# Two graph layers on one core: weight sums moved, background work spread differently, a bias added by DMA, and the layer boundary reordered

## The chip, the cores and the metric

The kernel runs on one core of a Trainium2 chip. Its time is what the device takes for one execution, in microseconds. A measurement is the median of a few executions. The profile and the trace come from one further execution, taken by the hardware profiler, whose own time stands beside its span in the table below.

A core has a matrix engine (TensorE, "PE" in the profile, its weight loads "PEld"), three engines for elementwise work (VectorE "DVE", ScalarE "ACT", GpSimd "POOL") and SyncE ("SP"), which here only issues DMAs. Each engine takes its own instructions in order. The engines meet through semaphores.

## The reference

There are N = 2708 rows of D = 1024 floats and an integer matrix adj of N x N. Both layers normalize first and add their result to x.

```python
# layer 0
h = jnp.maximum(_layernorm(x, axis=-1), 0.0)
f = h @ Wf + bf
g = h @ Wg + bg
e = jax.nn.relu(f @ g.T)
attention = jax.nn.softmax(jnp.where(adj > 0, e, NEG), axis=1)
x = x + attention @ (h @ W + bW)
# layer 1
h = jnp.maximum(_layernorm(x, axis=-1), 0.0)
k = h @ W1
f1 = k @ a1
f2 = k @ a2
e = leaky_relu(f1 + f2.T, 0.2)
attention = jax.nn.softmax(jnp.where(adj > 0, e, NEG), axis=1)
x = x + relu(attention @ k)
```

## The kernel before, in words

**Products.** All matrix products are float32. Each is computed with the Strassen-Winograd scheme: the operands are cut into 2 x 2 blocks, and seven products of half size (M1 to M7) of sums of blocks take the place of eight. The sums are made by DVE or POOL. The results are put together where PSUM is emptied, which is called an eviction. [...]

**Tiles.** The rows are 22 tiles, 20 of 128 rows and two of 74. They go in eleven pairs. The N rows of the output of a layer are also cut into five panels of 586, 586, 512, 512 and 512. Matrices are kept transposed, so a panel is a range of columns of a transposed score matrix, and every product has a half panel (293 or 256) or 512 as its free size.

**Stages of layer 0.** f and g are not computed. Wf times the transpose of Wg is folded into one matrix, and `project_q(p)` multiplies it with panel p of h. For each panel p, `scores(p)` then multiplies every pair of row tiles with that result. It writes seven products for a pair, adds the mask and keeps the running maximum. Then come `project_q(p+1)` and `aggregate(0, p)`, which multiplies the softmax weights with h, and `project(0, p)`, which multiplies by W and adds the residual. The order is broken at the end: `project(0, 3)` stands after `scores(4)`, and `project(0, 4)` comes last of layer 0, working on one pair after the other (`by_pair`).

**Stages of layer 1.** The scores need no matrix product. f1 and f2 are two dot products per row (`dots(0)`, `dots(1)`), made when a row of layer 0 is done. `mx[p]` collects the column maximum for panel p (`raise_max`, one DVE instruction for each row tile and panel). `shifts1(p)` makes of it the shift of the softmax: `column_max` turns `mx[p]` on TensorE, reduces it on DVE, and a chain of nine operations of 128 x 5 follows. `weights1(p)` spreads two results over the partitions (`spread`: transpositions on TensorE into PSUM and a copy out). For each row tile it then makes the weights P by an Identity on ACT (L1144), two operations on DVE and an Exp on ACT (L1147). Then `aggregate(1, p)` and `project(1, p)` follow for each panel.

**Masks.** While layer 0 computes its scores, adj is loaded as integers, converted by DVE (`convert`, tile nm), turned by TensorE (`turn`, mk_ps, L615), copied by ACT (L616) and stored to mk_d. Layer 1 loads masks from there.

**Order of the work.** A list named `later` holds background work with a nominal duration each: the layernorms, the sums of W, dots, maxima, softmax steps. `behind(rate)` stands in the products and lets as much of the list go as its credit pays for. `flush()` empties the list. In `scores` `behind` is called with seven rates for each pair, and the rate was 0.6 for panel 0 and 1.0 for the rest (L901). A scheduler then orders the instructions of each engine. It is bound to program order for SP's loads (`load`, L120), and for DVE inside `scores` alone (`nc.hold`). Nearly all DVE instructions show as L44, where a helper records them.

**Queues.** All loads are issued by SP in program order. All stores are issued by POOL. Buffers that loads share come from a ring of twelve (`stream`), others from a pool of 54 (`slot`). A load waits for what last used its buffer, and so do all loads behind it on SP.

**What the change touches.**
- `prepare_W` (called at L1110) puts eight pieces of work in the list. Each loads two rows of blocks of W (w_rows), makes four sums on DVE and stores them to wt_d (L775), and for layer 1 also makes four dot products.
- `finish0(p)`: `start` loads the residual x_res and adds the bias row bwb on POOL (L1078). `go` adds an evicted result (L1082) and stores the row to x1_d (L1083, "x_d" in the profile).
- `project`: M1 is copied out of PSUM by ACT (L827), M5 and M6 are added to it, and M3, M7 and M4 each take two DVE additions, one to the stored sum and one to the residual.
- `rows_done` for the last panel: it normalizes the row in place (ACT, L251), which must wait for the store of that row. It then makes both dots and the maximum.

Of the kernel before, what the change touches and what calls it, by code (L numbers as in the profile page):

```python
# [56 lines left out]
def kernel(  # L57
# [141 lines left out]
    def halves(t):  # L199
        return [t[:, e * W:(e + 1) * W] for e in range(2)]  # L200
# [38 lines left out]
        nc.scalar.activation(rs[:n, :1], mv[:n, 1:2], AF.Sqrt, bias=eps[:n])  # L239
        of_rows[id(t)] = mv, rs  # L240

    def normalize(t):

        n = t[0].shape[0]
        if id(t) not in of_rows:
            moments(t)
        mv, rs = of_rows.pop(id(t))
        nc.vector.reciprocal(rs[:n, :1], rs[:n, :1])
        nc.vector.tensor_scalar(rs[:n, 1:], mv[:n, :1], rs[:n, :1], -1.0, op0=OP.mult, op1=OP.mult)
        for e in range(2):  # L250
            nc.scalar.activation(t[e], t[e], AF.Relu, bias=rs[:n, 1:], scale=rs[:n, :1])  # L251

    def pair_h(l, q, ha, hb):

# [532 lines left out]
    def project(l, p, G, finish, then={}, by_pair=False, rate=2.0):  # L787

        full = width[p] // P
        col = lambda i, n: [t[:, :, i * P:i * P + n] for t in G]  # L790
        todo = [(first[p] + i, first[p] + i + 1, P, col(i, P), col(i + 1, P)) for i in range(0, full, 2)]
        if p == panel_of[short[0]]:
            n = tiles[short[0]][1]
            for e in range(2):
                nc.scalar.copy(carry[:, e, :, :n], G[e][:, :, full * P:full * P + n])
        if p == panel_of[short[1]]:
            n = tiles[short[1]][1]
            todo.append((*short, n, [carry[:, e, :, :n] for e in range(2)], col(full, n)))
        start_of, finish = finish
        ws = {m: load_W(l, m) for m in (M1, M2)}  # L800
        start_of([t for g in todo for t in g[:2]])
        lefts = []
        for ta, tb, n, (a11, a12), (a21, a22) in todo:
            s = [slot(f"ps{i}", (P, NH, P))[:, :, :n] for i in range(4)]
            add(s[0], a21, a22)
            sub(s[1], s[0], a11)
            sub(s[2], a11, a21)
            sub(s[3], a12, s[1])
            lefts.append({M1: a11, M2: a12, M5: s[0], M6: s[1], M7: s[2], M3: s[3], M4: a22})
        for group, left in (zip([[t] for t in todo], [[t] for t in lefts]) if by_pair else [(todo, lefts)]):  # L810
            acc, tmp = {}, {}
            for m in (M1, M2, M5, M6, M3, M7, M4):
                start = m in (M1, M5, M6)
                w_ = ws.pop(m) if m in ws else load_W(l, m)
                which = "x" if m in (M1, M2) else "y" if m in (M5, M3) else "z"
                for i, (ta, tb, n, _, _) in enumerate(group):
                    if start:
                        acc[which, i] = bank(f"p{which}")
                    ps = acc[which, i][:n]
                    for k in range(NH):  # L820
                        nc.tensor.matmul(ps, left[i][m][:, k, :], w_[k], start=(start and k == 0), stop=(k == NH - 1),  # L821
                                         skip_group_check=True)
                    if start:
                        tmp[m, i] = slot(f"pt{m}")
                    t = lambda m: tmp[m, i][:n, :W]
                    if m == M1:
                        nc.scalar.copy(t(M1), ps)  # L827
                    elif m == M2:
                        finish(ta, 0, ps)
                    elif m in (M5, M6):  # L830
                        add(t(m), ps, t(M1))
                    else:
                        o = {M3: M6, M7: M5, M4: M1}[m]
                        add(t(o), ps, t(o))
                        finish(tb if m != M3 else ta, 0 if m == M4 else 1, t(o))
                    behind(rate)
                if m in then:
                    then.pop(m)()
# [52 lines left out]
    def scores(p, B):  # L891
# [6 lines left out]
        spread(rb, [r_[:n, first[p] + i:first[p] + i + 1] for i, (_, n) in enumerate(panels[p])])  # L898
        acc = slot("acc")
        S = [None] * NT  # L900
        rate = 0.6 if p == 0 else 1.0  # L901
        lefts = {}

        def product(q, m, ps, start):
# [100 lines left out]
    def shifts1(p, between=None):  # L1005

        k, t0 = len(panels[p]), first[p]
        top = column_max(p, mx[p], between)[:, :k]
        f1 = f[0][:, t0:t0 + k]
        z, m, c = (stats.tile([P, 5], FP, name=nm)[:, :k] for nm in ("z", "m1", "none"))  # L1010
        nc.vector.tensor_add(z, f1, top)
        nc.vector.scalar_tensor_tensor(m, z, ALPHA, z, op0=OP.mult, op1=OP.max)
        nc.vector.tensor_scalar(c, top, -BIG / 2, None, op0=OP.is_ge)
        nc.vector.tensor_mul(m, m, c)
        nc.vector.tensor_scalar(c, top, -BIG / 2, -BIG, op0=OP.is_lt, op1=OP.mult)
        nc.vector.tensor_add(m, m, c)
        sub(z, f1, m)
        nc.vector.scalar_tensor_tensor(m, f1, ALPHA, m, op0=OP.mult, op1=OP.subtract)
        return z, m

    done_rows, first_mask = {}, {}

    def rows_done(t, xt):

        n = tiles[t][1]
        done_rows[t] = xt

        def dots(k):
            dot(f[k][:n, t:t + 1], xt, [b[:n] for b in halves(wab[k])])
            if k == 1:  # L1030
                nc.vector.tensor_scalar(f2s[:n, t:t + 1], f[1][:n, t:t + 1], ALPHA, None, op0=OP.mult)

        q, k = pair_of[t]
        whole = all(s in done_rows for s in pairs[q])
        if panel_of[t] == NP - 1:
            normalize(xt)
            dots(0)
            dots(1)
            raise_max(0, q, k, first_mask[t][:n, :width[0]])
            if whole and q == NQ - 1:  # L1040
                nc.scalar.activation(stats.tile([P, 1], FP, name="warm"), eps, AF.Exp)
            if whole:
                if q == NQ - 1:
                    got["zm"] = shifts1(0, lambda: pair_h(1, q, *(done_rows[s] for s in pairs[q])))
                else:
                    pair_h(1, q, *(done_rows[s] for s in pairs[q]))
                for p in range(1, NP):
                    put_max(p, q)
            return

        def met():
            known.add(q)
            for p in range(NP):
                if generated[p] > q:
                    put_max(p, q)
        put(1.5, lambda: moments(xt))
        put(0.5, lambda: normalize(xt))
        put(1.6, lambda: dots(0))
        put(1.6, lambda: dots(1))
        if whole:  # L1060
            put(2.7, lambda: pair_h(1, q, *(done_rows[s] for s in pairs[q])))
            put(0.0, met)

    def finish0(p):
        bwb = [slot(f"bwb{e}") for e in range(2)]
        for e in range(2):
            load(bwb[e][:, :W], bass.AP(tensor=bw.tensor, offset=bw.offset + e * W, ap=[[0, P], [1, W]]))
        xs, seen = {}, {}

        def start(ts):  # L1070
            for t in ts:
# [3 lines left out]
                xs[t] = row_halves("x_res", n, t in short)  # L1075
                for e in range(2):
                    load(xs[t][e], x[r0:r0 + n, e * W:(e + 1) * W])
                    nc.gpsimd.tensor_add(xs[t][e], xs[t][e], bwb[e][:n, :W])  # L1078

        def go(t, e, c):  # L1080
            n = tiles[t][1]
# [2 lines left out]
            seen[t] = seen.get(t, 0) + 1  # L1084
            if seen[t] == 2:
                rows_done(t, xs[t])
        return start, go

    got = {}
    generated = [0] * NP  # L1090

    def take_max(p):
        got["m"] = column_max(p, got["acc"])
# [6 lines left out]
    for p in range(NP):  # L1100
# [24 lines left out]
    project(0, NP - 1, G.pop(NP - 1), finish0(NP - 1), by_pair=True, rate=0.0)  # L1125


    def weights1(p, z, m):

        w = width[p]  # L1130
        ub, vb1, sm = slot("ub"), slot("vb1"), slot("sm")
        spread(ub, columns_of(p, z))
        spread(vb1, columns_of(p, m))
        S = [None] * NT
        order = [(q, k) for k in range(2) for q in range(NQ)]
        exps[0] = 0
# [1 line left out]
        def go(i, mk):  # L1138
            if i < len(order):
                q, k = order[i]  # L1140
                n, t = rows_of[q], pairs[q][k]
                S[t] = slot("P")
                s = S[t][:n, :w]
                nc.scalar.activation(s, vb1[:n, :w], AF.Identity, bias=f2s[:n, t:t + 1])  # L1144
                nc.vector.scalar_tensor_tensor(s, ub[:n, :w], f[1][:n, t:t + 1], s, op0=OP.add, op1=OP.max)
                add(s, s, mk[0][:n, :w])
                nc.scalar.activation(s, s, AF.Exp)  # L1147
            if i >= LAG:
                q, k = order[i - LAG]
# [3 lines left out]
        front = []  # L1153
        for i in range(len(order) + LAG):
            mk = []
            front.append([2.1, (lambda i=i, mk=mk: mk.append(load_mask(p, *order[i]))) if i < len(order) else None,
                          (lambda i=i, mk=mk: go(i, mk)), False, None])
        later[:0] = front
        return S, sm
# [1 line left out]
    def finish1(p):  # L1161
# [9 lines left out]
        def go(t, e, c):  # L1171
# [5 lines left out]
        return start, go  # L1177

    def take_shifts(p):
        flush()  # L1180
# [42 lines left out]
```

## Time and the profile before

| | |
|---|---|
| median of 3 executions | 3235.16 us (3231.14 to 3235.99) |
| profiled execution | 3237.23 us |
| its span | 3235.3 us |
| mean granted TensorE clock | 0.987 |
| PE busy | 3137.1 us (97%) |
| DVE busy | 1756.3 us (54%) |
| ACT busy | 507.7 us (16%) |
| POOL busy | 395.0 us (12%) |
| moved by DMA | 641.43 MB, mean 198 GB/s |

The busy shares are of the span. A group line of the profile gives the source line, the engine, the operation, output and input tiles, and shapes. A timeline line begins with the start and the duration in microseconds, and the bracket at its end gives the idle time of the engine just before it, and what ended that. A waits line gives the waiting instruction and what it waited for, the total in us, how often, and the longest. Where several matmuls follow one another, one timeline line holds them all.

### The profile page before, as it was taken

How to read it: one execution, taken by the hardware profiler on the slowest of the kernel's cores; microseconds unless marked ns; L12 is line 12 of the kernel's file. 1: busy time of each engine (PE TensorE's matmuls, PEld its weight loads, DVE VectorE, ACT ScalarE, POOL GpSimd, SP SyncE). 2: the span in 40 equal slices, each digit the busy share in tenths (PEclk: the TensorE clock that was granted, in tenths of full speed). 3: DMA queues.
4: the chain of work that ended last, by engine and by line, in shares of the span. 5: the costliest groups of instructions: out<-in, count | busy, mean ns of one | idle time of the engine just before them, and what ended most of it. 6: DMA issues, size and time to landing. Idle time of an engine off the chain costs nothing. (4 is left out here: it accounts for less than half of the span.)

```text
span 3235.3 us, 35363 instructions
## 1 busy us (share of the span) xinstructions
PE 3137.1 (97%) x12924; PEld 2333.4 (72%) x12924; DVE 1756.3 (54%) x3594; ACT 507.7 (16%) x853; POOL 395.0 (12%) x476
## 2 busy tenths in 40 slices
PE   8999999999999999999999998997999999999998
PEld 5577767667876578876888885864767748778585
DVE  7857594275812766327581358537574272553712
ACT  4412120010200102001020002003131030211200
POOL 3723110210002100021000101020010000000001
PEclk9999999999999999999999999998999999999999
DMA  6958866576445575457745565665555445555546
GB/s 262 332 174 297 276 229 227 171 243 215 141 130 163 173 247 190 151 191 242 228 156 156 165 209 185 225 237 200 198 161 175 148 159 171 186 189 175 194 150 212
DMA packets 279628, 641.43 MB, mean 198 GB/s; under 512 B 50686, under 2 KB 116178, under 8 KB 279456
## 3 DMA queue, kind: packets, MB, share of 16 engines
q1 hardware_dynamic: 245184, 525.56, 50.5%
q0 software_dynamic: 34272, 113.62, 9.4%
q8 instruction: 102, 1.67, 0.2%
q14 instruction: 70, 0.57, 0.1%
HBM read 525.49 MB, written 113.58 MB: 198 GB/s over the span
## 5 line engine op out<-in xcount | busy, mean ns | idle before, releaser
L917 PE MATMUL sz<-B,As 128*128 128x256 f32 (+3 forms) x1320 | 328.9, 399 | 5.3 <-DVE st L44 5.3
L917 PEld LDWEIGHTS sz<-B,As 128*128 128x128 f32 (+1 forms) x1320 | 248.7, 189 | 64.5 <-DVE st L44 6.4
L917 PE MATMUL sx<-B,As 128*128 128x256 f32 (+3 forms) x880 | 227.0, 401 | 14.2 <-DMA As<-hs_d 12.0
L756 POOL TENSOR_TENSOR gT<-gT,rr 128x2048 f32<-128x2048 f32 (+3 forms) x20 | 68.3, 3433 | 1320.5 <-DVE rr L44 700.2
L917 PE MATMUL sy<-B,As 128*128 128x256 f32 (+3 forms) x880 | 219.5, 392 | 0.0
L478 PE MATMUL gy<-T,hc 128*128 128x256 f32 (+3 forms) x880 | 205.7, 395 | 6.6 <-DMA hc<-hg_d 6.6
L478 PE MATMUL gx<-P,hc 128*128 128x256 f32 (+3 forms) x880 | 204.5, 394 | 4.7 <-ACT P L1147 4.7
L478 PE MATMUL gz<-Sa,hc 128*128 128x256 f32 (+3 forms) x880 | 206.6, 394 | 0.0
L478 PE MATMUL gz<-P,hc 128*128 128x256 f32 (+3 forms) x880 | 206.3, 393 | 0.0
L917 PEld LDWEIGHTS sx<-B,As 128*128 128x128 f32 (+1 forms) x880 | 162.3, 189 | 51.4 <-issue 11.2
L478 PEld LDWEIGHTS gy<-T,hc 128*128 128x128 f32 (+1 forms) x880 | 168.5, 192 | 42.3 <-DVE junk L44 4.4
L478 PEld LDWEIGHTS gx<-P,hc 128*128 128x128 f32 (+1 forms) x880 | 168.4, 192 | 40.9 <-ACT P L1147 5.0
L917 PEld LDWEIGHTS sy<-B,As 128*128 128x128 f32 (+1 forms) x880 | 163.9, 186 | 38.2 <-issue 0.9
L478 PEld LDWEIGHTS gz<-Sa,hc 128*128 128x128 f32 (+1 forms) x880 | 165.6, 190 | 31.8
L478 PEld LDWEIGHTS gz<-P,hc 128*128 128x128 f32 (+1 forms) x880 | 165.6, 190 | 31.8
L821 PE MATMUL px<-w,gT 128*128 128x512 f32 x320 | 147.3, 613 | 11.5 <-issue 10.0
L821 PE MATMUL py<-w,ps 128*128 128x512 f32 (+1 forms) x352 | 155.6, 593 | 0.3 <-DVE mcol L44 0.3
L821 PE MATMUL pz<-w,ps 128*128 128x512 f32 (+1 forms) x352 | 155.0, 592 | 0.0
L616 ACT COPY mask<-mk_ps 128x1024 bf16<-128x1024 bf16 (+1 forms) x55 | 55.6, 1011 | 575.8 <-PE mk_ps L615 254.6
L821 PEld LDWEIGHTS pz<-w,ps 128*128 128x128 f32 (+1 forms) x352 | 65.5, 186 | 85.6 <-issue 81.7
L821 PEld LDWEIGHTS py<-w,ps 128*128 128x128 f32 (+1 forms) x352 | 65.4, 186 | 85.6 <-issue 82.7
L821 PEld LDWEIGHTS px<-w,gT 128*128 128x128 f32 x320 | 62.5, 197 | 89.2 <-issue 85.3
(240 smaller groups left out, 4797.9 us busy)
## 6 DMA issues: line engine op xcount, KB each, us to landing
hc<-hg_d SPq DMA_DIRECT2D x350, 512.0 KB
As<-hs_d SPq DMA_DIRECT2D x150, 512.0 KB
w<-wt_d SPq DMA_DIRECT2D x96, 512.0 KB
w<-in_L_gnn_W_dram SPq DMA_DIRECT2D x72, 512.0 KB
md<-md_d SPq DMA_DIRECT2D x56, 512.0 KB
adj_i<-in_adj_dram SPq DMA_DIRECT2D x50, 512.0 KB
hg_d<-g POOLq DMA_DIRECT2D x40, 512.0 KB, 5.0
hs_d<-hsT POOLq DMA_DIRECT2D x40, 512.0 KB, 5.6
```

The source lines that it names most:

```text
L478: nc.tensor.matmul(ps[d], left(m, k, d), right(m, k), start=(start and k == 0), stop=(k == K - 1), skip_group_check=True)
L616: nc.scalar.copy(mk[:n, :, :k4 * P], ps[:n, :, :k4 * P])
L756: nc.gpsimd.tensor_tensor(of(e, s), of(e, s), by(s, k), OP.mult)
L821: nc.tensor.matmul(ps, left[i][m][:, k, :], w_[k], start=(start and k == 0), stop=(k == NH - 1), skip_group_check=True)
L917: nc.tensor.matmul(ps[:n, :h], lefts[q][:, i % 2, c, :n], B[m][c // 2][:, c % 2, :h], start=(start and c == 0), stop=(c == NH - 1), skip_g ...
```

## The change

1. `prepare_W` is called after M5 of `aggregate(0, 0)` instead of before that stage.
2. The rate in `scores` is 0.6, 1.0, 0.65, 0.65, 0.65 for the five panels instead of 0.6 and four times 1.0.
3. The bias row bW is not loaded to SBUF and added by POOL. Each x_res tile gets it by a DMA from POOL's queue that reads the row from DRAM for all partitions and adds it to what the tile holds.
4. In `project` of layer 0, as soon as M6 is there, `join` adds the three sums of M5, M6 and M1 to the residual tiles. M3, M7 and M4 are then added to the residual straight from PSUM. In the last panel M1 is copied by DVE instead of ACT.
5. In the last panel `normalize` writes into fresh tiles (h_last) instead of in place. `raise_max` stands between `dots(1)` and `dots(0)`. The small Exp that loads ACT's table is kept in program order ahead of them.
6. `scores_before` spreads f1 of panel 0 and makes, as background work behind `project(0, 3)`, the unshifted masked scores of panel 0 for the first tile of those nine pairs whose rows are both done by then. `weights1(0)` then subtracts the shift from these and applies Exp; the rest is made as before. `shifts1` returns this shift m as well.

```diff
-    def normalize(t):
+    def normalize(t, into=None):
...
-            nc.scalar.activation(t[e], t[e], AF.Relu, bias=rs[:n, 1:], scale=rs[:n, :1])
+            nc.scalar.activation((into or t)[e], t[e], AF.Relu, bias=rs[:n, 1:], scale=rs[:n, :1])
...
-        start_of, finish = finish
+        start_of, join, finish = finish
...
+        copy1 = nc.vector.tensor_copy if by_pair and l == 0 else nc.scalar.copy
...
+                    o = {M3: M6, M7: M5, M4: M1}.get(m)
                     if m == M1:
-                        nc.scalar.copy(t(M1), ps)
+                        copy1(t(M1), ps)
                     elif m == M2:
                         finish(ta, 0, ps)
-                    elif m in (M5, M6):
+                    elif o is None:
                         add(t(m), ps, t(M1))
-                    else:
-                        o = {M3: M6, M7: M5, M4: M1}[m]
+                    elif join is None:
                         add(t(o), ps, t(o))
                         finish(tb if m != M3 else ta, 0 if m == M4 else 1, t(o))
+                    else:
+                        finish(tb if m != M3 else ta, 0 if m == M4 else 1, ps)
+                    if join and m == M6:
+                        join(tb, 1, t(M5))
+                        join(ta, 1, t(M6))
+                        join(tb, 0, t(M1))
                     behind(rate)
...
-        rate = 0.6 if p == 0 else 1.0
+        rate = (0.6, 1.0, 0.65, 0.65, 0.65)[p]
...
         if panel_of[t] == NP - 1:
-            normalize(xt)
-            dots(0)
+            done_rows[t] = row_halves("h_last", n)
+            normalize(xt, done_rows[t])
+            if whole and q == NQ - 1:
+                tc.keep_in_program_order(nc.scalar.activation(stats.tile([P, 1], FP, name="warm"), eps, AF.Exp))
             dots(1)
             raise_max(0, q, k, first_mask[t][:n, :width[0]])
-            if whole and q == NQ - 1:
-                nc.scalar.activation(stats.tile([P, 1], FP, name="warm"), eps, AF.Exp)
+            dots(0)
...
-                    nc.gpsimd.tensor_add(xs[t][e], xs[t][e], bwb[e][:n, :W])
+                    nc.gpsimd.dma_start(xs[t][e], bass.AP(tensor=bw.tensor, offset=bw.offset + e * W, ap=[[0, n], [1, W]]),
+                                        accum_op=OP.add)
...
+        def join(t, e, c):
+            add(xs[t][e], xs[t][e], c)
+        return start, join, go
...
+    def scores_before():
+
+        w = width[0]
+        f1b = slot("f1b")
+
+        def go(q, mk):
+            n, t = rows_of[q], pairs[q][0]
+            before[t] = slot("P")
+            s = before[t][:n, :w]
+            nc.scalar.activation(s, f1b[:n, :w], AF.Identity, bias=f2s[:n, t:t + 1], scale=ALPHA)
+            nc.vector.scalar_tensor_tensor(s, f1b[:n, :w], f[1][:n, t:t + 1], s, op0=OP.add, op1=OP.max)
+            add(s, s, mk[0][:n, :w])
+        spread(f1b, columns_of(0, f[0]))
+        for q in range(NQ):
+            if panel_of[pairs[q][0]] < NP - 1 and panel_of[pairs[q][1]] < NP - 1:
+                mk = []
+                put(1.8, lambda q=q, mk=mk: go(q, mk), lambda q=q, mk=mk: mk.append(load_mask(0, q, 0)))
...
             project(0, p - 1, G.pop(p - 1), finish0(p - 1), hooks)
-        if p == 0:
-            prepare_W()
-        then = {}
+            scores_before()
+        then = {M5: prepare_W} if p == 0 else {}
...
+        if p == 0:
+            mb = slot("mb")
+            spread(mb, columns_of(p, shift))
+        else:
+            spreads()
...
-                S[t] = slot("P")
-                s = S[t][:n, :w]
-                nc.scalar.activation(s, vb1[:n, :w], AF.Identity, bias=f2s[:n, t:t + 1])
-                nc.vector.scalar_tensor_tensor(s, ub[:n, :w], f[1][:n, t:t + 1], s, op0=OP.add, op1=OP.max)
-                add(s, s, mk[0][:n, :w])
+                if p == 0 and t in before:
+                    S[t] = before.pop(t)
+                    s = S[t][:n, :w]
+                    sub(s, s, mb[:n, :w])
+                else:
+                    if p == 0 and not spreaded:
+                        spreads()
+                        spreaded.append(True)
...
                 nc.scalar.activation(s, s, AF.Exp)
```

More of the change, by code (lines that the diff above doesn't have):

```diff
@@ L1009, in shifts1 @@
         f1 = f[0][:, t0:t0 + k]
-        z, m, c = (stats.tile([P, 5], FP, name=nm)[:, :k] for nm in ("z", "m1", "none"))
+        z, m, c, d = (stats.tile([P, 5], FP, name=nm)[:, :k] for nm in ("z", "m1", "none", "m2"))
         nc.vector.tensor_add(z, f1, top)
+        nc.vector.tensor_scalar(c, top, -BIG / 2, None, op0=OP.is_ge)
+        nc.vector.tensor_scalar(d, top, -BIG / 2, -BIG, op0=OP.is_lt, op1=OP.mult)
         nc.vector.scalar_tensor_tensor(m, z, ALPHA, z, op0=OP.mult, op1=OP.max)
-        nc.vector.tensor_scalar(c, top, -BIG / 2, None, op0=OP.is_ge)
         nc.vector.tensor_mul(m, m, c)
-        nc.vector.tensor_scalar(c, top, -BIG / 2, -BIG, op0=OP.is_lt, op1=OP.mult)
-        nc.vector.tensor_add(m, m, c)
+        nc.vector.tensor_add(m, m, d)
         sub(z, f1, m)
-        nc.vector.scalar_tensor_tensor(m, f1, ALPHA, m, op0=OP.mult, op1=OP.subtract)
-        return z, m
+        nc.vector.scalar_tensor_tensor(c, f1, ALPHA, m, op0=OP.mult, op1=OP.subtract)
+        return z, c, m
     done_rows, first_mask = {}, {}
@@ L1028, in dots @@
         def dots(k):
-            dot(f[k][:n, t:t + 1], xt, [b[:n] for b in halves(wab[k])])
+            dot(f[k][:n, t:t + 1], done_rows[t], [b[:n] for b in halves(wab[k])])
             if k == 1:
@@ L1064, in finish0 @@
     def finish0(p):
-        bwb = [slot(f"bwb{e}") for e in range(2)]
-        for e in range(2):
-            load(bwb[e][:, :W], bass.AP(tensor=bw.tensor, offset=bw.offset + e * W, ap=[[0, P], [1, W]]))
         xs, seen = {}, {}
@@ L1086, in go @@
                 rows_done(t, xs[t])
-        return start, go
+        def join(t, e, c):
+            add(xs[t][e], xs[t][e], c)
+        return start, join, go
     got = {}
     generated = [0] * NP
+    before, spreaded = {}, []
+    def scores_before():
[13 more added lines that the diff above has]
+                put(1.8, lambda q=q, mk=mk: go(q, mk), lambda q=q, mk=mk: mk.append(load_mask(0, q, 0)))
     def take_max(p):
@@ L1125, with weights1, spreads @@
     project(0, NP - 1, G.pop(NP - 1), finish0(NP - 1), by_pair=True, rate=0.0)
-    def weights1(p, z, m):
+    def weights1(p, z, m, shift):
         w = width[p]
         ub, vb1, sm = slot("ub"), slot("vb1"), slot("sm")
-        spread(ub, columns_of(p, z))
-        spread(vb1, columns_of(p, m))
+        def spreads():
+            spread(ub, columns_of(p, z))
+            spread(vb1, columns_of(p, m))
+        if p == 0:
[3 more added lines that the diff above has]
+            spreads()
         S = [None] * NT
@@ L1141, in go @@
                 n, t = rows_of[q], pairs[q][k]
-                S[t] = slot("P")
-                s = S[t][:n, :w]
-                nc.scalar.activation(s, vb1[:n, :w], AF.Identity, bias=f2s[:n, t:t + 1])
-                nc.vector.scalar_tensor_tensor(s, ub[:n, :w], f[1][:n, t:t + 1], s, op0=OP.add, op1=OP.max)
-                add(s, s, mk[0][:n, :w])
+                if p == 0 and t in before:
[6 more added lines that the diff above has]
+                        spreaded.append(True)
+                    S[t] = slot("P")
+                    s = S[t][:n, :w]
+                    nc.scalar.activation(s, vb1[:n, :w], AF.Identity, bias=f2s[:n, t:t + 1])
+                    nc.vector.scalar_tensor_tensor(s, ub[:n, :w], f[1][:n, t:t + 1], s, op0=OP.add, op1=OP.max)
+                    add(s, s, mk[0][:n, :w])
                 nc.scalar.activation(s, s, AF.Exp)
@@ L1155, in weights1 @@
             mk = []
-            front.append([2.1, (lambda i=i, mk=mk: mk.append(load_mask(p, *order[i]))) if i < len(order) else None,
+            front.append([2.1, (lambda i=i, mk=mk: mk.append(load_mask(p, *order[i])))
+                          if i < len(order) and not (p == 0 and pairs[order[i][0]][order[i][1]] in before) else None,
                           (lambda i=i, mk=mk: go(i, mk)), False, None])
@@ L1176, in go @@
             nc.gpsimd.dma_start(out[r0:r0 + n, e * W:(e + 1) * W], xs[t][e])
-        return start, go
+        return start, None, go
     def take_shifts(p):
```

## The prediction

> **What bounds the kernel now.** The busy line of the page comes first, then TensorE's waits, then the same stretches as windows, then single lines of the timeline.
>
> ```profile
> PE 3137.1 (97%) x12924; PEld 2333.4 (72%) x12924; DVE 1756.3 (54%) x3594; ACT 507.7 (16%) x853; POOL 395.0 (12%) x476
> ```
>
> TensorE is busy 97% of the span, and the change takes no product away. So only 3235.3 - 3137.1 = 98 us of idle time can be won, and what a lowered clock adds after a stop. The waits say where:
>
> ```profile
> PE mk_ps L615 <- DVE nm L44: 17.0, 9, 3.4
> PE mx_ps L654 <- DVE mx L44: 14.8, 1, 14.8
> PE sx L917 <- DMA As<-hs_d: 12.0, 4, 4.3
> PE px L821 <- issue: 10.0, 3, 4.8
> PE gy L478 <- DMA hc<-hg_d: 6.6, 2, 4.0
> PE sz L917 <- DVE st L44: 5.3, 2, 4.9
> PE gx L478 <- ACT P L1147: 4.7, 1, 4.7
> ```
>
> (us in total, times, longest.) They lie in five places, as windows show:
>
> ```profile
> 452.00:500.00 48.00, 41.39 (x156) 30.78 (x155) 39.92 (x104) 1.61 (x4) 12.96 (x24) 0.93 1.00 375
> 1119.00:1200.00 81.00, 73.01 (x343) 59.21 (x342) 59.20 (x121) 6.88 (x8) 8.01 (x11) 0.94 0.74 236
> 1486.00:1530.00 44.00, 37.22 (x180) 29.18 (x179) 37.78 (x84) 6.95 (x9) 9.06 (x13) 0.96 0.83 269
> 1940.00:1960.00 20.00, 15.07 (x68) 12.56 (x67) 13.69 (x13) 1.01 (x1) 10.54 (x9) 0.91 0.72 254
> 2150.00:2236.00 86.00, 57.93 (x137) 26.83 (x136) 55.04 (x131) 15.51 (x24) 10.54 (x18) 0.83 0.73 248
> ```
>
> After the width come PE, PEld, DVE, ACT and POOL busy, then the granted clock, the DMA share and GB/s. I price a place as idle time (width less PE busy) plus PE busy times what the clock lacks. Aggregate(0,0): 6.6 + 2.9 = 9.5 us. Scores of panel 2: 8.0 + 4.4 = 12.4. Scores of panel 3: 6.8 + 1.5 = 8.3. Scores of panel 4: 4.9 + 1.4 = 6.3. Layer boundary: 28.1 + 9.8 = 37.9. Together 74 us: this is the pot.
>
> The lines behind three of the places:
>
> ```profile
> 1942.98 9.81 POOL L1078 TENSOR_TENSOR x_res<-x_res,bwb 128x512 f32<-128x512 f32 x8
> 1944.85 8.50 DVE L44 SCALAR_TENSOR_TENSOR Sb<-Sb,mask 128x512 f32<-128x512 f32 x1
> 1954.46 3.68 PE L917 MATMUL sz<-B,As 128*128 128x256 f32 x8 [4.93 <-DVE st L44]
> ...
> 2185.16 6.11 PE L821 MATMUL px<-w,gT 128*128 128x512 f32 x8 [4.83 <-issue]
> ...
> 2211.38 0.54 POOL L1083 DMA_DIRECT2D x_d<-x_res  x1 [4.40 <-DVE f2s L44]
> 2217.47 0.81 ACT L251 ACTIVATE x_res<-x_res,rs 128x512 f32<-128x512 f32 x1 [3.06 <-DMA x_d<-x_res]
> 2223.42 1.33 PE L654 MATMUL mx_ps<-ident,mx 128*128 128x128 f32 x5 [14.80 <-DVE mx L44]
> ```
>
> One DVE operation, 0.69 us elsewhere, lasts 8.50 while POOL adds biases, and TensorE stops for 4.93. At the boundary the second normalize waits 3.06 for the store of the row that it overwrites.
>
> **The Trainium skill.** "SBUF — State Buffer", Who interferes with whom: a VectorE operation with two SBUF inputs and a GpSimd operation that reads SBUF exclude each other. The 8.50 against 0.69 agrees. "TensorE: Matmul & The Clock Gate", Part 1: the clock halves after about 3.4 us idle and needs about as long to recover. The trace agrees: px took 6.11 after 4.83 idle, 3.60 normally. "DMA: Bandwidth & Descriptors", SWDGE vs HWDGE vs iDMA: accumulation exists on GpSimd's queue alone; and its Anatomy of one DMA gives 2.0 us plus bytes by 436 GB/s. For 256 KB this is an estimate of 2.6 us; the trace's plain x_d stores of that size take 3.8, which I use. No run yet shows an accumulating one.
>
> **The change part by part**, against the profiled execution's 3237.23 us (span 3235.3); the median of the runs is 2.1 lower.
>
> *prepare_W after M5 of aggregate(0,0).* Before, M5's hc loads stand on SP behind w_rows loads whose stream buffers come free only as POOL's wt_d stores land (6.5 us each); M5 waits 2.60 and 4.01. After, the twelve hc loads of M1 and M5 and two of M2 are issued ahead of the first eight w_rows. All of them still move: the DMA share is 1.00 here, and 4 MB of rows with 4 MB of stores beside M2's and M6's hc is some 8 MB in 17 us, above the 375 GB/s shown. So hc may be late in M2 instead, by an estimated 2 to 6 us. I take -5, ends -9 (all gone) and +2.
>
> *Rates 0.65 in scores of panels 2 to 4.* A pair calls for seven nominal us of background; now 4.55. In the loaded stretch of panel 2 DVE was 35.5 us busy in 39 (11.8 per 13 us); in a quiet one, 6.6 in 13. Taking 2.45 off leaves about 9.4 of a pair's 12.6 us on PE, so a mask conversion (nm) finds DVE free. Not all goes: the instruction order still puts three mask transpositions per panel early, after M2 instead of after M3 (in panel 2 pairs 1, 5, 6 instead of 2, 3, 4; in panel 3 pairs 1, 4, 5 instead of 1, 2, 3), and one wait of 2.8 us is for As. Panel 2: -9 of 12.4. Panel 3: -5 of 8.3. Ends: half of each, or all. The unspent work runs in the aggregates, where a product of 18.8 us needs four PSUM evictions from DVE; their windows outside those above show no such waits, so I cost this at nothing. If that cover is short, flush meets the rest at the boundary (below).
>
> *Bias by DMA.* Away go 44 POOL adds of 1.26 us (54.0 us of POOL, mostly beside PE) and ten bwb loads. In come 44 accumulating DMAs, 0.54 us of POOL's queue each by the x_d row, and 11.3 MB against 2.6. Worth: the lock in panel 4, -6 of 6.3. New wait: DVE's first residual operation in each project waits for a landing, and behind it in DVE's queue stand PSUM evictions for which PE waits. Slack: the POOL adds end 15.1, 11.9, 11.4, 27.4 and 11.5 us before the first finish. An eight-issue train of 4.3 plus a landing at 3.8 to 8 (twice the plain one) ends 8 to 12 us after its start, about as the 9.8 of adds did: nothing. Stores queued on POOL behind the train wait at most those 4.3 us, as they did behind the adds. Ends 0 and +65 (rival).
>
> *Boundary.* (a) The second pair's M1 copy moves from ACT to DVE, and for one pair M5, M6 and M1 are joined into the residual at M6, so the last three products finish with one DVE operation each. px waited 4.83 because its bank's ACT copy came late (2184.50), then ran 6.11. On DVE it stands behind the first pair's dots: I estimate it ends at 2186.7, but PE has M1, M5 and a quarter of M6 to do, so 2.5 us of stop and no slow clock: -4.7. (b) From the last product's end (2208.6) to gx (2233.85) it was 25.25 us. After: one residual add, bn, aggregate, square root, reciprocal and two relus into the fresh h_last, no 3.06 us store wait; dots(1) and raise_max ahead of dots(0) (two junk operations and their ends, about 1.7, off the path): the maximum is ready about 7 after the end. Reductions behind 2.5 of left-over DVE work, small operations 1.0, spread of mb 1.2, copy 0.6, subtract 0.75, Exp 0.7 with its table kept loaded (the load took 1.28): about 15. So -10. Its ends: -8 and -18 for (a) and (b) together; I take -15. (c) PE does five more transpositions for f1b, +1.1. Nine panel-0 scores made in aggregate(0,4) cost DVE 9 x 1.5 us there beside 130 us of products: hidden.
>
> *Unseen.* +2 for small waits in new places.
>
> Sum: -5 - 9 - 5 - 6 - 15 + 1 + 2 = -37, to 3200 for a profiled run and 3198 for the median.
>
> **Rivals.** *Partial.* The hc wait only moves to M2 (0), early masks keep the scores at half (-6), the boundary gives -8 and panel 4 -6: about -17, 3218. For it: the DMA share of 1.00 and the unchanged three early masks per panel. Against: DVE's 91% there is what is cut. *Slower: late landing.* The accumulating train takes over some 22 us from first issue (adds' start to first finish: 24.9, 26.6, 21.3, 37.2, 21.4). From there each us is paid in each project: at 35 us, about 13 x 5 = 65, less 35 of gains, is +30: 3265. It decides from 22 + 37/5, about 29 us. For it: nothing in this trace shows such a DMA's time. Against: 3.8 us landings of plain ones. *The end does not move.* Left-over dots and sums ahead of the reductions eat the boundary, and the scores stay as they are, since DVE's order decides: only panel 4 is won, -6: 3229, no change.
>
> **How the numbers follow.** A measurement here tells about 0.2%, 6.5 us, from no change. Forecast 0.54, 3183 to 3212 (ends of the parts, in part together). Partial 0.28, 3208 to 3227. No move 0.06. Late landing or another slower wait 0.12. The range 3183 to 3225 leaves out the slower case, most of no move and the tails. Faster 0.82, same 0.06, slower 0.12.
>
> **What would show it.** DVE's 8.50 at panel 4 gone, and no TensorE wait for st; mk_ps <- nm falling from 17.0 to below 10 with nothing left in panel 2 or 3 over 2; gy <- hc gone, or gx or gz <- hc in its place; mx_ps <- mx at about 7 to 9 instead of 14.8; gx <- P about 3. Wrong if DVE shows idle time before x_res released by a DMA of bW, or if the five windows sum to more than 50 us of loss.

## The result and the profile after

The kernel after takes 3196.61 us (median of 5, 3196.38 to 3199.18). The kernel before takes 3233.49 us in the same comparison. The ratio is 0.9889, with a 95% interval of 0.9875 to 0.9902, so 36.9 us less. The forecast was 3198. The profiled execution took 3196.38 us, with a span of 3194.6. The one of before, 3237.23, lies 3.7 above its median, so the spans differ by a little more, 40.7 us.

From the profile page after, the busy line:

```profile
PE 3124.2 (98%) x12934; PEld 2327.1 (73%) x12934; DVE 1757.6 (55%) x3606; ACT 507.7 (16%) x853; POOL 380.3 (12%) x476
```

TensorE's idle time fell from 98.2 to 70.4 us, by 27.8. Its busy time fell from 3137.1 to 3124.2, by 12.9, although it has ten matmuls more. That is time no longer spent at a lowered clock: in the five places below the clock's part of the loss falls from 20.0 to 9.4 us. Idle and busy time together make up the 40.7 us.

TensorE's waits after. Here hc are the blocks of h that a product of `aggregate` reads, As those that `scores` reads, st and sm sums of score products, pt sums of `project`:

```profile
PE px L822 <- issue: 11.1, 3, 5.8
PE sx L924 <- DMA As<-hs_d: 9.2, 3, 4.5
PE mk_ps L615 <- DVE nm L44: 8.8, 7, 2.5
PE mx_ps L654 <- DVE mx L44: 7.1, 1, 7.1
PE gx L478 <- DMA hc<-hg_d: 6.7, 2, 5.9
```

Against before: mk_ps fell from 17.0 to 8.8 and mx_ps from 14.8 to 7.1, while sz <- st nearly went (5.3 to 0.7). The wait for hc did not go. It moved from gy (M5) to gx (M2). And px <- issue grew from 10.0 to 11.1.

The same five places as windows of the kernel after (width, PE, PEld, DVE, ACT, POOL busy, clock, DMA share, GB/s):

```profile
460.00:520.00 60.00, 53.28 (x207) 40.15 (x206) 28.40 (x68) 1.61 (x4) 10.78 (x20) 0.94 0.69 249
1105.00:1190.00 85.00, 83.62 (x426) 69.94 (x425) 71.35 (x149) 10.64 (x13) 13.02 (x18) 1.00 0.85 278
1470.00:1535.00 65.00, 60.94 (x309) 49.48 (x308) 54.52 (x116) 9.26 (x12) 9.84 (x15) 1.00 0.84 271
1910.00:1960.00 50.00, 50.00 (x190) 33.96 (x189) 33.23 (x63) 7.36 (x11) 9.62 (x12) 1.00 0.88 268
2119.98:2195.00 75.02, 56.41 (x135) 25.79 (x134) 51.23 (x126) 10.56 (x17) 10.54 (x18) 0.89 0.91 302
```

Priced as in the prediction (idle, plus PE busy times what the clock lacks), the losses are:

| place | before | after |
|---|---|---|
| aggregate(0,0) | 9.5 | 9.9 |
| scores, panel 2 | 12.4 | 1.4 |
| scores, panel 3 | 8.3 | 4.1 |
| scores, panel 4 | 6.3 | 0 |
| layer boundary | 37.9 | 24.8 |

Their sum falls by 34 us. A stop of 2.7 us in project(0,3), which the prediction had not listed, is gone too. Before, it stood here:

```profile
2007.82 8.83 PE L821 MATMUL pz<-w,gT 128*128 128x512 f32 x16 [2.74 <-DVE pt L44]
```

The lines of the timeline after that matter below:

```profile
510.88 6.37 PE L478 MATMUL gx<-Sb,hc 128*128 128x293 f32 x16 [5.90 <-DMA hc<-hg_d]
...
1925.12 7.04 POOL L1083 DMA_DIRECT2D x_res<-in_L_gnn_bW_dram  x8 [0.54 <-DVE sm L44]
1948.76 0.69 DVE L44 TENSOR_TENSOR x_res<-x_res,pt 128x512 f32<-128x512 f32 x1 [3.92 <-DMA x_res<-in_L_gnn_bW_dram]
...
2149.17 1.02 PE L822 MATMUL py<-w,ps 128*128 128x512 f32 x2
2155.25 0.68 DVE L44 COPY pt<-px 128x512 f32<-128x512 f32 x1
2156.04 5.88 PE L822 MATMUL px<-w,gT 128*128 128x512 f32 x8 [5.84 <-issue]
2186.89 1.33 PE L654 MATMUL mx_ps<-ident,mx 128*128 128x128 f32 x5 [7.06 <-DVE mx L44]
2194.50 22.02 PE L478 MATMUL gx<-P,hc 128*128 128x293 f32 x88
```

Read them so: hc stops M2 for 5.90. An accumulating DMA makes DVE wait 3.92, with PE unhindered. The second pair's px waits for a copy that DVE makes only at 2155.25.

### The profile page after: what moved, and what is told of

It is laid out like the page before. It is cut to its first block, busy times and chain, and to the rows that moved or that the text cites. A ratio compares the mean times of both kernels' runs of the same rounds, so it can differ in the third digit from the quotient of the medians.

```text
span 3194.6 us, 35414 instructions
## 1 busy us (share of the span) xinstructions
PE 3124.2 (98%) x12934; PEld 2327.1 (73%) x12934; DVE 1757.6 (55%) x3606; ACT 507.7 (16%) x853; POOL 380.3 (12%) x476
## 4 chain that ended last, share of the span: by engine, by line
PE 83%; issue 8%; DVE 4%; POOL 2%; DMA 2%; ACT 1%; SPq 0%; POOLq 0%; DVEq 0%; ACTq 0%
PE gz L478 13%; PE gy L478 13%; PE gx L478 12%; PE sz L924 8%; PE sy L924 5%; PE sx L924 5%; PE pz L822 5%; PE gv L478 4%; PE M_ps L413 3%; PE qz L478 3%; PE py L822 3%; PE px L822 3%; PE qy L478 2%; PE qx L478 2%; PE mk_ps L615 1%
## 5 line engine op out<-in xcount | busy, mean ns | idle before, releaser
L822 PE MATMUL px<-w,gT 128*128 128x512 f32 x320 | 145.5, 607 | 12.5 <-issue 11.1
```

## The experiments

The first four runs put one part of the change each into the kernel before. All ratios are against the kernel before, timed beside each run; its medians were 3233.5 to 3233.7. Where a run is compared with after, the two medians come from separate comparisons, which this agreement allows.

### The weight sums later, alone

```diff
-        if p == 0:
-            prepare_W()
-        then = {}
+        then = {M5: prepare_W} if p == 0 else {}
```

> The kernel before with one edit: the sums of W are put in the list after M5 of aggregate(0,0). Theory: the traces of before and after show the stop at hc leaving M5 (6.6 us, gy) and coming back in M2 (6.7 us, gx), so this edit alone gives 0 to -1 us against before. Rival, as the prediction had it: the stop in M5 goes and only part of it returns, -3 to -7 us. In the profile: gy <- hc gone, gx <- hc about 6 us in M2 of aggregate(0,0).

Measured: 3231.18 us, ratio 0.9993 (0.9985 to 1.0001). TensorE's waits in aggregate(0,0) of this run:

```profile
PE gx L478 <- DMA hc<-hg_d: 5.8, 2, 4.5
```

Before, the wait in M5 was 6.6. The stop has changed its product, not gone, and the gain can't be told from none. Of the rival's range only the end at -3 to -4.9 is left.

### The rates, alone

```diff
-        rate = 0.6 if p == 0 else 1.0
+        rate = (0.6, 1.0, 0.65, 0.65, 0.65)[p]
```

> The kernel before with one edit: the rate in scores of panels 2 to 4 is 0.65 instead of 1.0. Theory: DVE's surplus is what delays nm, so this edit alone gives what the traces show in the scores of panels 2 and 3, -11 and -4, about -15 us; panel 4 keeps its 8.50 us DVE operation and the 4.9 us stop. Rival: part of it came from the POOL adds or from the shifted order of the earlier work, then -5 to -9 and mk_ps <- nm keeps over 12 us in all.

Measured: 3223.29 us, ratio 0.997 (0.9959 to 0.9982), 10.3 us less. Two of TensorE's waits, and the windows of panels 2 and 3:

```profile
PE mk_ps L615 <- DVE nm L44: 9.9, 8, 2.5
PE sz L917 <- DVE st L44: 5.9, 3, 5.2
```

```profile
1105.00:1190.00 85.00, 83.60 (x421) 69.93 (x420) 71.78 (x152) 9.63 (x12) 12.84 (x18) 1.00 0.84 279
1470.00:1535.00 65.00, 60.32 (x291) 47.17 (x290) 54.58 (x123) 9.88 (x14) 12.19 (x18) 1.00 0.80 264
```

mk_ps falls to 9.9 and panel 2 loses 1.4 us, as in the kernel after: the rates did that. The lock in panel 4, the long DVE operation beside POOL's additions, stays (sz 5.9). The time saved lies between theory (15) and rival (5 to 9). The two windows lose 14.6 us less than before, as the theory said. But in M5 of aggregate(0,0), ahead of anything the edit touches, TensorE stood 8.9 us in this profile against 6.6 before, so at least part of the difference is not the edit's.

### The bias by DMA, alone

```diff
-                    nc.gpsimd.tensor_add(xs[t][e], xs[t][e], bwb[e][:n, :W])
+                    nc.gpsimd.dma_start(xs[t][e], bass.AP(tensor=bw.tensor, offset=bw.offset + e * W, ap=[[0, n], [1, W]]),
+                                        accum_op=OP.add)
```

The loads of bwb go as well.

> The kernel before with one edit: the bias row is added to x_res by accumulating DMAs of POOL's queue, without the bwb loads and POOL's adds. Theory: it takes away the lock in the scores of panel 4 alone, -6 us (-5 to -8). Rival: the accumulating DMAs land late (12.4 us median and 21.2 at most after their issue in the profile of after), and with the longer DVE chain of the kernel before they reach the path: 0 or slower, with DVE idle before its first residual operation.

Measured: 3218.7 us, ratio 0.9959 (0.9945 to 0.9972), 14.9 us less. Both theories are wrong: the gain is twice the expected one. TensorE's waits for st and pt went from 5.3 and 5.1 to 0.4 and 2.4, so the stop in project(0,3) went with this edit too. DVE never waited for one of these DMAs in this run.

### The boundary edits, alone

The edit is all of the parts 4 to 6 of the change, with the old rates, bias and place of the weight sums.

> The kernel before with the edits of project and of the layer boundary together (early join, M1 copied by DVE in the last panel, h_last, the new order of dots, scores of panel 0 made ahead); rates, bias and place of the weight sums as before. Theory: the boundary gives the 11 us that the traces differ by there, and the join takes one DVE addition from the end of project(0,3), where 4.6 us of stop went: -15 us together (-11 to -17). Rival: the stop in project(0,3) went by the rates or the bias, then -9 to -11.

Measured: 3221.85 us, ratio 0.9964 (0.9951 to 0.9978), 11.7 us less, between the two expectations. Its executions spread from 3213.6 to 3225.3, and the profiled one is the fastest. The other four were not profiled. The timeline of the fast one differs from before here:

```profile
1937.16 10.78 POOL L1086 TENSOR_TENSOR x_res<-x_res,bwb 128x512 f32<-128x512 f32 x8
1939.03 1.20 DVE L44 SCALAR_TENSOR_TENSOR Sb<-Sb,mask 128x512 f32<-128x512 f32 x1
1940.26 1.64 DVE L44 TENSOR_TENSOR acc<-acc,Sb 128x512 f32<-128x512 f32 x1
1995.69 7.13 PE L822 MATMUL pz<-w,gT 128*128 128x512 f32 x16 [3.32 <-DVE x_res L44]
```

Here DVE got in between POOL's eight additions, with 1.20 and 1.64 us instead of 8.50. So whether the lock comes depends on how the two engines meet, and this can be why that execution was fast. And the stop in project(0,3), now 3.32, is there without the long lock.

### M1 of the last panel copied by ACT

```diff
-        copy1 = nc.vector.tensor_copy if by_pair and l == 0 else nc.scalar.copy
+        copy1 = nc.scalar.copy
```

> The kernel after with one edit: M1 of the last panel is copied out of PSUM by ACT again. Theory: in after the copy stands on DVE behind the first pair's dots and sums and ends at 2155.93, while ACT is free from 2149.93 on since its relus no longer wait for a store. So px no longer waits 5.84 us and does not run 5.88 us at the lowered clock: -6 to -9 us against after, about 3189. Rival: the DVE work that the copy stood behind only moves to the end, in front of the last maximum (mx_ps <- mx grows from 7.1), and the gain is 0 to -3.

Measured: 3188.47 us, ratio 0.9863 (0.9849 to 0.9876), 8.1 us less than after. Its timeline at the second pair:

```profile
2147.91 0.56 ACT L829 COPY pt<-px 128x512 f32<-128x512 f32 x1
2148.57 3.67 PE L822 MATMUL px<-w,gT 128*128 128x512 f32 x8 [0.30 <-issue]
```

The wait is 0.30 instead of 5.84, and px runs 3.67 instead of 5.88. mx_ps <- mx stayed at 7.0, so nothing came back at the end. The move of the copy to DVE was a loss inside the change.

### Each accumulating DMA twice

```diff
+                    for _ in range(2):
-                    nc.gpsimd.dma_start(xs[t][e], ..., accum_op=OP.add)
+                        nc.gpsimd.dma_start(xs[t][e], ..., accum_op=OP.add)
```

> The kernel after with each accumulating DMA of the bias issued twice; the bias row is so added twice. Theory: a landing came at 23.6 us after the train's first issue once (project(0,3)) and cost DVE 3.9 us but PE nothing; with twice as many in line the trains take 15 to 25 us longer, and PE stops in most of the five projects: slower by 10 to 60 us than after, with DVE waiting for the DMA of bW. Rival: the landings are long only because loads beside them take the DMA engines, or there is more slack than that; then within 3 us of after.

Measured: 3215.62 us, ratio 0.9947 (0.9935 to 0.996), 19.0 us more than after. DVE waited for these DMAs nine times, 77.5 us in all and 17.1 at most. Where that reaches PE, the timeline shows:

```profile
1966.60 0.69 DVE L44 TENSOR_TENSOR x_res<-x_res,pt 128x512 f32<-128x512 f32 x1 [17.12 <-DMA x_res<-in_L_gnn_bW_dram]
1972.27 9.52 PE L822 MATMUL py<-w,ps 128*128 128x512 f32 x16 [8.33 <-DVE pt L44]
```

In the same project pz waits another 4.38. In project(0,2) DVE waited 16.3, but PE only 0.85; in project(0,4) a load of W came 2.48 late, which was not followed up. So late landing is a real way to lose time, but in one project, not in most of them: it is project(0,3) that stops.

### The weight sums at half the density

```diff
-                put(2.7 if l == 0 else 8.0, ...
+                put(5.4 if l == 0 else 8.0, ...
```

> The kernel after with one edit: the nominal duration of the first four weight sums in the list is 5.4 instead of 2.7 us, so they are loaded and stored in twice the time. Theory: hc is late in M2 of aggregate(0,0) because its loads stand on SP behind w_rows whose ring buffers wait for stores, in a burst; spread out, the 6.7 us stop goes, -5 to -8 us against after, about 3190. Rival: it is the order of the loads, not their density; then the stop stays at 4 to 7 us, or moves to a later product, and the time is as after.

Measured: 3187.61 us, ratio 0.9865 (0.985 to 0.988), 9.0 us less than after. The window of aggregate(0,0):

```profile
460.00:520.00 60.00, 59.38 (x242) 45.42 (x241) 23.19 (x52) 3.23 (x8) 9.16 (x17) 1.00 0.71 260
```

PE is busy for 59.38 of 60 us, against 53.28 in after. SP's loads and one window, first in after and then in this run:

```profile
457.63 25.99 SPq L121 DMA_DIRECT2D w_rows<-in_L_gnn_W_dram  x8
487.24 4.28 SPq L121 DMA_DIRECT2D hc<-hg_d  x2
502.56 0.41 SPq L121 DMA_DIRECT2D hc<-hg_d  x1
495.00:511.00 16.00, 10.10 (x42) 7.48 (x40) 12.75 (x32) 0.00 (x0) 7.45 (x14) 0.92 0.98 380
```

```profile
455.88 18.09 SPq L121 DMA_DIRECT2D w_rows<-in_L_gnn_W_dram  x6
477.59 8.22 SPq L121 DMA_DIRECT2D hc<-hg_d  x3
495.00:511.00 16.00, 16.00 (x67) 12.31 (x66) 7.36 (x15) 1.15 (x3) 4.94 (x10) 1.00 1.01 382
```

In after eight loads of rows stand together and hold SP for 25.99 us, with hc behind them; here six, for 18.09. By the matmuls done until then, M2 stops for the third hc load behind the rows. It was issued at 502.56 in after; here the third was out by 485.8. From 495 to 511 us the DMA engines move as much in both runs, 380 and 382 GB/s, and only after has a stop. So what counts is how early that load is issued, not how much moves beside it: the lower density helps by changing the order on SP, which the rival had named. The order alone, at the old density, was not tried.

### No scores made ahead

```diff
-            scores_before()
```

> The kernel after without the scores of panel 0 made ahead: weights1(0) makes all of them at the boundary, with both spreads ahead of the first as before. Theory: the time from the shift to the first matmul of layer 1 grows by the second spread (1.2), the Identity and two DVE operations (2.1) less the one subtraction (0.75): +2 to +4 us against after. Rival: DVE cannot keep up with TensorE at the start of aggregate(1,0) without the nine scores, and PE stops there again and again: +6 to +15.

Measured: 3202.61 us, ratio 0.9905 (0.9891 to 0.9918), 6.0 us more than after. One wait came back, a single time, as TensorE's waits show:

```profile
PE gx L478 <- ACT P L1188: 4.4, 1, 4.4
```

After it, the first gx product took 24.73 us for its 88 records, against 22.02 in after: 2.7 us of lowered clock. The stop has the place that the theory gave it, not the rival's many stops. Its cost is larger than expected for two reasons. The clock was left out. And this kernel still spreads mb, which nothing in it reads: ACT copies mb at 2188.96 and comes to ub only at 2189.94. So 6.0 is too much for the scores by an estimated 1 us, from these two starts.

### Both improvements

These are the copy by ACT and the weight sums at half the density, in the kernel after.

> The kernel after with both edits that were faster alone: M1 of the last panel copied by ACT, and a nominal 5.4 us for each of the first four weight sums. Theory: the two stops lie 1600 us apart and each goes by its own cause, so the gains add up: 8 and 9 us less than after, about 3180. Rival: one takes what the other would have taken (a later wait absorbs it), then 3185 to 3188.

Measured: 3181.59 us (3180.45 to 3183.42), ratio 0.9837 (0.9824 to 0.9851). This is 15.0 us less than after, where 8.1 and 9.0 would add up to 17.1; the difference is within the intervals. It is the fastest version here.

### The bias by DMA in project(0,3) alone

```diff
+                    if p == 3:
+                        nc.gpsimd.dma_start(xs[t][e], ..., accum_op=OP.add)
+                    else:
                         nc.gpsimd.tensor_add(xs[t][e], xs[t][e], bwb[e][:n, :W])
```

In this project the loads of bwb go as well.

> The kernel before with the bias added by DMA in project(0,3) alone; the other four projects keep POOL's adds and their bwb loads. Theory: the 8 us by which the lock delays DVE at 1944.85 persist, since DVE has no slack through the softmax steps of project(0,3), and cause the stop of 2.7 us there too; so this one project is worth nearly all of the bias edit, -10 to -14 us against before. Rival: the stop in project(0,3) or the other projects' adds have causes of their own, then -6 to -8 and the rest of the 14.9 lies in the other four.

Measured: 3226.37 us (3217.92 to 3227.29), ratio 0.9968 (0.9956 to 0.9981), 7.3 us less. The window over panel 4's end and project(0,3), of this run and then of the kernel before:

```profile
1930.00:2030.00 100.00, 100.00 (x363) 66.85 (x363) 82.55 (x188) 25.53 (x42) 15.92 (x23) 1.00 0.73 231
```

```profile
1940.00:2020.00 80.00, 71.58 (x211) 39.66 (x210) 68.13 (x117) 19.52 (x31) 15.44 (x18) 0.96 0.54 180
```

Before, 8.4 us of this stretch were idle and some 3 more lost to the clock; here nothing is. So both stops hang on this one project's additions. The median gain, 7.3 (6.1 to 14.2), nevertheless lies where the rival had it; the profiled execution took 3221.7, 12.0 less. The theory's cause for the second stop, DVE's persisting delay, does not hold, since the boundary run had the stop without the long lock. What differs in the program is the scheduler's order of DVE's instructions in project(0,3):

```text
with POOL's additions               with the DMA
mcol <- mx_ps                       eight sums ps
eight sums ps                       mcol <- mx_ps
nine Sa <- Sa,mb                    x_res <- px,x_res (twice, bn between)
x_res <- px,x_res                   five Sa <- Sa,mb
eight more subtractions of mb       pt <- py,pt
and x_res <- px,x_res               ...
pt <- py,pt                         ...
```

With the additions, the evictions of PSUM stand further behind softmax steps. DVE also idles ahead of mcol, with the eight sums still behind it, first before and then in this run:

```profile
1968.94 0.88 DVE L44 TENSOR_REDUCE mcol<-mx_ps 128x1 f32<-128x128 f32 x4 [5.30 <-PE mx_ps L654]
1958.34 0.89 DVE L44 TENSOR_REDUCE mcol<-mx_ps 128x1 f32<-128x128 f32 x4 [0.23 <-PE mx_ps L654]
```

The boundary run has 5.23 there. That this order makes the stop is read from it, not tried by itself. The spread of this run's executions (9.4 us) leaves open how much of the bias edit's 14.9 us belongs to the other four projects.

### Fresh tiles for the normalized rows, alone

```diff
-            normalize(xt)
+            done_rows[t] = row_halves("h_last", n)
+            normalize(xt, done_rows[t])
...
```

> The kernel before with one edit: in the last panel normalize writes to fresh tiles h_last, so it does not wait for the store of the row. Order of dots, join, copy and scores as before. Theory: the waits of 3.32 and 3.06 us for the store go from the path; the first also delayed the moments, relus and the ACT copy of the second pair, for which px waited 4.83: -6 to -9 us against before, over half of the boundary's gain. Rival: DVE's order is what counts, the store wait covers DVE work that then takes its place: 0 to -3.

Measured: 3225.06 us, ratio 0.9971 (0.9959 to 0.9982), 8.6 us less. The timeline of the profiled execution, the slowest of the six (3229.32):

```profile
2182.43 0.56 ACT L827 COPY pt<-px 128x512 f32<-128x512 f32 x1
2183.09 3.67 PE L821 MATMUL px<-w,gT 128*128 128x512 f32 x8 [1.86 <-issue]
2215.16 1.33 PE L654 MATMUL mx_ps<-ident,mx 128*128 128x128 f32 x5 [11.03 <-DVE mx L44]
```

px waits 1.86 instead of 4.83 and runs at full clock, and the maximum comes 3.8 us earlier. Alone it gives 8.6 us (5.8 to 13.3), where all the boundary edits together gave 11.7 (7.1 to 15.8). The further 4 us by which the maximum comes earlier in after (7.06) belong to the early join and the new order of dots and maximum; no run parts these two.

### POOL's additions put back into the kernel after

The loads of bwb come back too.

> The kernel after with the bias added by POOL again (bwb loads and 44 adds), all else as in after. Theory: the lock in the scores of panel 4 and DVE's delay come back whatever the rates are: +9 to +15 us against after. Rival: with the lower rates and one DVE addition less DVE has the slack to take the lock, then +2 to +7 and the 14.9 us of the bias edit alone belong in part to the other edits as well.

Measured: 3208.81 us, ratio 0.9921 (0.9907 to 0.9934), 12.2 us more than after. The timeline:

```profile
1925.27 8.51 DVE L44 SCALAR_TENSOR_TENSOR Sb<-Sb,mask 128x512 f32<-128x512 f32 x1
1934.89 3.78 PE L924 MATMUL sz<-B,As 128*128 128x256 f32 x8 [4.94 <-DVE st L44]
1989.60 7.13 PE L822 MATMUL pz<-w,gT 128*128 128x512 f32 x16 [3.32 <-DVE x_res L44]
```

Lower rates do not shield DVE from the lock, and both stops are back.

## Why the prediction was right, and where its steps were not

The time was within 2 us of the forecast. That closeness is luck in part, since the terms erred in both directions:

| part | forecast | alone, on the kernel before |
|---|---|---|
| weight sums later | -5 | -2.4 (-4.9 to +0.3) |
| rates | -14 | -10.3 (-13.3 to -5.8) |
| bias by DMA | -6 | -14.9 (-17.8 to -9.1) |
| boundary, with f1b | -14 | -11.7 (-15.8 to -7.1) |
| unseen waits | +2 | |
| sum | -37 | -39.3, whole change -36.9 |

(The intervals are those of the ratios, times 3233.5.)

The signs that it named came in the main, with two exceptions. gx did not wait for P at all. And DVE did stand idle before x_res for a DMA of bW, which was to be a sign of being wrong: the landing was indeed longer than assumed, but TensorE did not stop there.

**Weight sums.** The step failed by taking a middle between "gone" and "moved". The prediction had itself said that hc might be late in M2 by 2 to 6 us; it was, by 6.7 in two waits, and the place lost 9.9 us where it had lost 9.5. Its reason, some 8 MB in 17 us, is not the whole of it. In after the DMA engines were 0.48 busy from 465 to 495 us, while SP stood behind loads of rows that waited for buffers which products still read, and the same 380 GB/s afterwards stopped nothing in the run with half the density. The step left out what stands ahead of hc on SP; the run that changed it gave 9.0 us.

**Rates.** The mechanism holds. Panel 2 kept 1.4 of 12.4 us where 3.4 was forecast, and panel 3 kept 4.1 in after where 3.3 was forecast. The early mask transpositions still wait there, 3.0 us in three waits in both the rates run and the kernel after, as the prediction's reason for a rest said.

**Bias.** Mis-sized by a factor of over two. The lock went as priced. The step that failed counted only this stop and put nothing down for what else would change in project(0,3). With the additions gone the scheduler orders DVE's work there otherwise, and a stop of 2.7 us with its lowered clock went as well. The landing was mis-sized the other way: 3.8 to 8 us was assumed, and the issues took 7.0 instead of 4.3. (The bytes are 11.1 MB, not 11.3.) The list of DMA issues (KB each, median us to landing) has:

```profile
x_res<-in_L_gnn_bW_dram POOLq DMA_DIRECT2D x40, 256.0 KB, 12.4
```

The longest was 21.2; the plain store's median is 4.6. The slack of project(0,3), 27.4 us, was taken from before's order, but the early join of the same change asks for the tiles sooner: DVE first touched one 18.2 us after the first issue, and its wait ended at 23.6. The rival of late landing had the way of the loss right, and doubling the train shows its cost. It had the number of projects wrong: this project alone was at its limit, and of the others project(0,2) lost 0.85 us to twice the train, while the cause of the 2.48 in project(0,4) is open.

**Boundary.** The tail from the last product's end to the first gx was forecast at 15 us. It is 14.7 (2179.8 to 2194.50), and the maximum was ready 7.06 after the end, forecast 7. The step that failed is (a), -4.7 for the copy on DVE. It assumed that PE had all of M5 and a quarter of M6 to do before px. In the program's order it has a quarter of M5 only (the line of two records at 2149.17), which is the first pair's order misapplied to the second. The kernel before has the same quarter there, two records at 2179.31. So px waited 5.84 and not 2.5, and kept its slow clock: 8.1 us lost with the clock, where before lost 7.3. The gain there came from h_last, whose end of the store waits freed ACT, the engine from which the copy was taken.

**Scores made ahead.** Their gain was inside the 15 us of the tail and was not priced by itself. It is 6.0 at most, with the clock after the stop in it, and about 5 without the needless spread.

## What to carry to other kernels

When a store wait is taken off an engine, look again at what had been moved away from that engine because of it: here the copy belonged back on ACT, for 8 us. A load that is late in one product may only be late in the next when other loads are moved; look at what then stands ahead of it in its queue. And when a concurrent operation is removed, the scheduler's order of another engine may change far from it, so compare the orders before costing the rest at nothing.

## What the runs showed of the hardware that was not expected

An accumulating DMA of 256 KB into SBUF, mostly in trains of eight, landed 12.4 us after its issue (median, from 5.2 to 21.2), against a median of 4.6 for a plain store of that size from the same queue in the same run. How much of that is waiting behind the others of its train was not measured. Its issue took POOL 0.88 us by the train of eight in 7.04, against 0.54 to 0.60 for a plain store. Whether a DVE operation is shut out by a train of eight POOL additions is a matter of how they meet: 8.50 and 8.51 us in two kernels, 1.20 and 1.64 in another. And whether a stop lowers the clock is not a matter of its length alone: the 16 matmuls of pz in project(0,3) took 8.83 us after a stop of 2.74 before, but 7.13 after 2.74 in the rates run and after 3.32 in the boundary run. So no idle time that the prediction quotes for this is a threshold here.
